# Linear attention and dense experts: one block of down projections per batch in place of two

## The chip, the cores and the metric

The kernel runs on one core of a Trainium2 chip. The metric is the device time of one execution in microseconds (us). TensorE (PE) multiplies matrices, VectorE (DVE), ScalarE (ACT) and GpSimd (POOL) work element by element, and SyncE (SP) mostly issues transfers. Each engine works through its own queue in the order in which the program issues instructions to it, and waits on semaphores for what other engines produce.

## What is computed

For each of 8 batches of 512 tokens with 128 channels (float32):

```python
x = x + layernorm(attention(layernorm(x)))
x = x + layernorm(experts(layernorm(x)))
# attention: k = softmax over tokens; context = k^T v per head; out = q context, then w_out, bias, residual
# experts, for each of 8, with 512 hidden channels:
h = silu(x @ wg) * (x @ wu)
acc = acc + h @ wd
```

No expert is routed: all eight are summed for every token, which is most of the arithmetic.

## The kernel before, in words

The order of all instructions is written out by hand: what the Python code issues first stands first in its engine's queue.

**Steps.** The experts of a batch are cut into 32 steps (8 experts, 4 tiles of 128 hidden channels each). A step is two matmuls of 512 tokens, g (L902) and u (L903), a silu on ScalarE (L905) and a product on VectorE that writes h (L926). g and u have two PSUM banks each. Batch 0 begins with two units of sixteen steps on half of the tokens (256 columns), and then runs steps 16 to 31 on all of them; in the half steps every third step uses the accumulators' banks. The last batch ends with steps 24 to 31 in two halves.

**Down projections.** Steps are taken in pairs, and a 2 by 2 product of a pair is formed with seven block products in place of eight (a Strassen scheme). GpSimd forms sums of the weights once per expert (`weight_sums`, L755) and differences of h for each pair (L940 to L942). The products are matmuls with 64 output channels, two of them side by side (L797, in `down_pairs`), and add up in two banks, accA and accB. `down_pairs` issues a whole block of them: one for the first eight pairs of a batch and one for the rest, each two steps behind its last pair (`LAG`). A batch has two blocks (the last batch one of eight pairs and one of four).

**Work beside the steps.** `plan` gives to each step a list of calls, which are issued behind its product. They prepare the next batches: the first norm of x (`stats`, `scales`, `norm`), its turn to channels (`turn`), the scaling by gamma and beta (`affine`, L493), the keys' product and softmax (`keys`, L501 to L508), the context in four pieces (`context`), the values and the second part of the attention (`values` to `residual`), the norm before the experts and its turn (`stats4` to `turn4`). They also finish the batch before: `Last` turns both accumulators back (`turn`), adds them up (`add`), normalizes and stores (`norm`). A turn is a transpose of 32 by 32 blocks on VectorE (L282, L291, L570), a transfer to DRAM (L270) and four transfers back (L275), all issued by SP. Powers for the norms are GpSimd's (L237, and L238 after it).

**Opening and end.** `opening` runs batch 0's attention by hand in two halves of tokens; its later pieces come from the generator `after_m`, whose second half goes on during the first half steps (the calls `go` in `plan`): statistics, covariance (L648 to L655) with its power (L658), the normalized y with the addition that gives x2 (L661), z from it (L252), the transposes of z (L261). `keep_warm` issues matmuls that nobody reads (L161). `End.finish` normalizes the last half from PSUM and stores it in two pieces.

## Time and profile before

| what | value |
|---|---|
| median of 3 runs | 693.56 us (693.36 to 693.69) |
| the profiled execution | 693.51 us |
| its span in the profile | 691.6 us |
| HBM traffic over the span | 30.82 MB, 45 GB/s |
| transfers to landing: turn out, turn back, x | 2.0 to 2.2, 2.0, 2.8 us |

The profile counts time from the first instruction of its span; the execution has 1.9 us around it. A line of a group or a timeline gives engine, source line, operation, what it writes and reads, partitions by elements, and how often. A matmul of float32 appears as two passes, so a row "x2" of g or u is one matmul. In timelines the first column is the start, the second the duration, both in us, and brackets name the idle time before a row and what ended it; since matmuls overlap, their cost is read from start to start.

### The profile page before, as it was taken

What the parts mean: (1) busy time and instruction counts of PE and PEld (TensorE: products, weight loads), DVE (VectorE), ACT (ScalarE), POOL (GpSimd) and SP (SyncE); (2) the same over time, 40 slices, a digit from 0 to 9 for tenths busy, and PEclk for the clock granted to TensorE, in tenths of its full rate; (3) what the DMA queues carried; (4) which work ended last, traced back from release to release, by engine and by line L of the source; (5) the groups of instructions that cost most, each with busy time, mean ns of one, the idle gap of its engine ahead of it and who ended that gap; (6) DMA issues with size and microseconds to landing.
All of it is one profiled execution on the core that took longest, in us unless ns stands there. A gap on an engine that the chain in (4) does not pass through costs nothing.

```text
span 691.6 us, 9214 instructions
## 1 busy us (share of the span) xinstructions
PE 682.9 (99%) x3175; PEld 374.3 (54%) x3175; DVE 298.3 (43%) x810; ACT 247.9 (36%) x475; POOL 424.6 (61%) x524
## 2 busy tenths in 40 slices
PE   9999999999999999999999999999999999999997
PEld 6786455454554545545455544545445454544576
DVE  6656433543236432563325624256332534134135
ACT  4552441433424333344332434244351423122221
POOL 4779773767548574495726766377673857546521
PEclk9999999999999999999999999999999999999999
DMA  8610201020010200102001010111001010010010
GB/s 265 196 31 1 76 20 58 16 93 0 31 61 1 92 0 31 61 16 78 0 31 61 30 65 0 51 41 57 22 16 63 14 47 1 1 61 1 15 55 24
DMA packets 36672, 30.82 MB, mean 45 GB/s; under 512 B 3985, under 2 KB 28049, under 8 KB 36625
## 3 DMA queue, kind: packets, MB, share of 16 engines
q1 hardware_dynamic: 36336, 30.03, 13.5%
q8 instruction: 25, 0.41, 0.2%
q10 hardware_dynamic: 288, 0.20, 0.1%
q14 instruction: 23, 0.18, 0.1%
HBM read 18.42 MB, written 11.80 MB: 44 GB/s over the span
## 4 chain that ended last, share of the span: by engine, by line
PE 96%; DVE 1%; ACT 1%; DMA 0%; issue 0%; POOL 0%; DVEq 0%; ACTq 0%
PE g L902 32%; PE u L903 31%; PE accA L797 16%; PE accB L797 12%; PE y_ps L528 1%; PE g_ps L443 1%; PE k_ps L501 1%; PE end L699 1%; DMA x<-in_L_attn_x_dram 0%; PE end_A L699 0%; ACT xh L245 0%; PE wa_ps L464 0%; PE end_B L699 0%; PE m_ps L458 0%; PE c_ps L452 0%
## 5 line engine op out<-in xcount | busy, mean ns | idle before, releaser
L926 DVE TENSOR_TENSOR h<-sg,u 128x512 f32<-128x512 f32 (+1 forms) x264 | 172.6, 655 | 352.0 <-PE u L903 340.4
L905 ACT ACTIVATE sg<-g 128x512 f32<-128x512 f32 (+1 forms) x280 | 156.3, 560 | 377.7 <-PE g L902 353.8
L902 PE MATMUL g<-zT,wg 128*128 128x512 f32 (+1 forms) x560 | 267.5, 559 | 1.4 <-ACT sg L905 0.7
L903 PE MATMUL u<-zT,wu 128*128 128x512 f32 (+1 forms) x560 | 265.7, 556 | 0.9 <-DVE h L926 0.9
L940 POOL TENSOR_TENSOR t<-h 128x512 f32<-128x512 f32 x124 | 157.2, 1268 | 158.4 <-DVE h L926 158.4
L903 PEld LDWEIGHTS u<-zT,wu 128*128 128x128 f32 x560 | 106.1, 190 | 115.2 <-issue 109.5
L902 PEld LDWEIGHTS g<-zT,wg 128*128 128x128 f32 x560 | 101.2, 190 | 98.9 <-issue 95.6
L797 PE MATMUL accB<-t,ws 128*64 128x256 f32 x496 | 138.2, 381 | 0.0
L797 PE MATMUL accA<-h,wd 128*64 128x256 f32 x496 | 128.1, 381 | 0.0
L941 POOL TENSOR_TENSOR t<-h,t 128x256 f32<-128x256 f32 x124 | 90.1, 726 | 9.7
L942 POOL TENSOR_TENSOR t<-h,t 128x256 f32<-128x256 f32 x124 | 90.0, 726 | 9.7
L797 PEld LDWEIGHTS accA<-h,wd 128*64 128x64 f32 x496 | 66.6, 137 | 45.2 <-issue 6.4
L797 PE MATMUL accB<-h,ws 128*64 128x256 f32 x248 | 73.8, 379 | 0.0
L797 PE MATMUL accA<-t,ws 128*64 128x256 f32 x248 | 73.8, 379 | 0.0
L797 PEld LDWEIGHTS accB<-t,ws 128*64 128x64 f32 x496 | 66.6, 137 | 0.0
L237 POOL TENSOR_TENSOR rstd<-ve,mhalf 128x4 f32<-128x4 f32 (+1 forms) x28 | 32.8, 1173 | 18.4 <-DVE nm L229 16.3
L797 PEld LDWEIGHTS accB<-h,ws 128*64 128x64 f32 x248 | 34.0, 137 | 17.9
L797 PE MATMUL accB<-t,wd 128*64 128x256 f32 x124 | 36.9, 379 | 0.0
L797 PE MATMUL accA<-t,wd 128*64 128x256 f32 x124 | 36.9, 379 | 0.0
L797 PEld LDWEIGHTS accA<-t,ws 128*64 128x64 f32 x248 | 34.0, 137 | 0.0
L797 PEld LDWEIGHTS accB<-t,wd 128*64 128x64 f32 x124 | 17.0, 137 | 9.0
L516 POOL TENSOR_TENSOR x<-x,bias_sb 128x128 f32<-128x128 f32 x28 | 11.9, 455 | 15.3 <-ACT x L245 15.3
(177 smaller groups left out, 414.3 us busy)
## 6 DMA issues: line engine op xcount, KB each, us to landing
wg<-in_L_ffn_Wg_dram SPq DMA_DIRECT2D x8, 256.0 KB, 6.0
wu<-in_L_ffn_Wu_dram SPq DMA_DIRECT2D x8, 256.0 KB, 5.9
wd<-in_L_ffn_Wd_dram SPq DMA_DIRECT2D x8, 256.0 KB, 6.1
bounce<-f_blkA SPq DMA_DIRECT2D x8, 256.0 KB, 2.0
fA<-bounce SPq DMA_DIRECT2D x32, 64.0 KB, 2.0
bounce<-f_blkB SPq DMA_DIRECT2D x8, 256.0 KB, 2.1
fB<-bounce SPq DMA_DIRECT2D x32, 64.0 KB, 2.0
x<-in_L_attn_x_dram SPq DMA_DIRECT2D x7, 256.0 KB, 2.8
```

The source lines that it names most:

```text
L237: nc.gpsimd.tensor_tensor(rstd, ve, mhalf[:, :n], ALU.pow)
L443: nc.tensor.matmul(g_ps[:, :C], xh[:, j, :], ek[:, :, j * Q : (j + 1) * Q], start=(j == 0), stop=(j == NJ - 1),)
L501: nc.tensor.matmul(k_ps, w_qkv_sb[:, C : 2 * C], self.xnT, start=True, stop=True)
L516: nc.gpsimd.tensor_tensor(self.x1[:, j], self.x1[:, j], bias_sb, ALU.add)
L797: nc.tensor.matmul(o, w, r, start=start, stop=stop)
L902: nc.tensor.matmul(g_ps[:, :cols], wg_sb[e][:, w], zT, start=True, stop=True)
L903: nc.tensor.matmul(u_ps[:, :cols], wu_sb[e][:, w], zT, start=True, stop=True)
L905: nc.scalar.activation(sg[:, :cols], g_ps[:, :cols], AF.Silu)
L926: nc.vector.tensor_tensor(flat(h), sg[:, :cols], u_ps[:, :cols], ALU.mult)
L940: nc.gpsimd.tensor_tensor(t2[:, 0:2], h2[:, 1::2], h2[:, 0:2], ALU.subtract)
L941: nc.gpsimd.tensor_tensor(t2[:, 2], h2[:, 3], t2[:, 0], ALU.subtract)
L942: nc.gpsimd.tensor_tensor(t2[:, 3], h2[:, 2], t2[:, 2], ALU.subtract)
```

## The change

The sixteen pairs of a batch are now all kept (`hp` has 16 buffers for h), and `down_pairs` issues them in one block directly behind step 31 (behind step 23 in the last batch). The differences are formed by a new function `differences`, which writes one of its four results over a part of h that is not read any more; ten pairs are formed during the steps (`EARLY`), the other six inside the block. New in the block are calls of `meanwhile`: the softmax of batch b + 2, the sum, statistics and norm of the batch before, and the bias of batch b + 2. The keys' product of batch b + 2 stands between step 31 and the block; in batch 0 its affine does too. To make room, tiles that had buffers of their own share them (x has two buffers in place of three; y, z, fn, the scratch tiles of turns and others use tags of tiles that are done), and x is loaded later.

The plans change with it: in batch 0 the pieces of the second half move by a step or two, all eight weight sums go to GpSimd at steps 2 to 8 and 10, the softmax of batch 1 goes one step behind its product, and the preparation of batch 2 goes to steps 20 to 30. In the opening, the statistics of batch 1 are issued in single pieces and their moments and powers ahead of m, and the first half of y and z get a bank per piece. In the end, ScalarE subtracts from the mean while the power is formed, and one operation on VectorE scales and adds.

```diff
-    xp = ctx.enter_context(tc.tile_pool(name="xp", bufs=3))
+    xp = ctx.enter_context(tc.tile_pool(name="xp", bufs=2))
+    x2p = ctx.enter_context(tc.tile_pool(name="x2p", bufs=3))
...
-    hp = ctx.enter_context(tc.tile_pool(name="hp", bufs=4))
-    pairp = ctx.enter_context(tc.tile_pool(name="pairp", bufs=9))
+    hp = ctx.enter_context(tc.tile_pool(name="hp", bufs=16))
+    tp = ctx.enter_context(tc.tile_pool(name="tp", bufs=10))
...
+        after = attentions[1] = Attention(1)
+        after.s = bn(after.x[:, :1], "1_1")
...
             nc.vector.tensor_reduce(kmax[:, h : h + 1], k_ps[h][:, :W], AX.X, ALU.max, negate=True)
+            if h == 0:
+                bn(after.x[:, 1:2], "1_1", after.s, 1)
...
+        bn(after.x[:, 2:3], "1_1", after.s, 2)
...
-        after = attentions[1] = Attention(1)
-        after.s = bn(after.x[:, :3], "1_1")
+        bn(after.x[:, 3:], "1_1", after.s, 3)
...
-        bn(after.x[:, 3:], "1_1", after.s, 3)
+        after.sc = scales(after.s, "1_1", pair=True)
+        m = work.tile([P, C], F32, tag="ctxT", name="m_0")
+        ms.append(m)
         nc.vector.tensor_scalar(m, m_ps[:, :C], rsum, None, ALU.mult)
         next(first)
...
-        moment = moments(after.s, "1_1", pair=True)
...
-        after.sc = powers(*moment, "1_1")
...
-        next(first)
...
         def keys(self):
+            self.product()
+            self.softmax()
+
+        def product(self):
             b = self.b
             k_ps = ps.tile([P, N], F32, tag="ps", name=f"k_ps_{b}")
             nc.tensor.matmul(k_ps, w_qkv_sb[:, C : 2 * C], self.xnT, start=True, stop=True)
             kmax = small.tile([P, 1], F32, tag="kmax", name=f"kmax_{b}")
             nc.vector.tensor_reduce(kmax, k_ps, AX.X, ALU.max, negate=True)
-            ekT = work.tile([P, N], F32, tag="ekT", name=f"ekT_{b}")
+            self.k = k_ps, kmax
+
+        def softmax(self):
+            b = self.b
+            k_ps, kmax = self.k
+            ekT = flat(work.tile([P, NQ, P], F32, tag="xhT", name=f"ekT_{b}"))
             ksum = small.tile([P, 1], F32, tag="ksum", name=f"ksum_{b}")
             nc.scalar.activation(ekT, k_ps, AF.Exp, bias=kmax, accum_out=ksum)
...
-        pool, tag = (ps_gu, "u") if lo else (ps, "ps")
-        y_ps = pool.tile([P, N], F32, tag=tag, name=f"y_ps_0_{lo}")
...
+        if lo:
+            y_ps = ps_gu.tile([P, N], F32, tag="u", name=f"y_ps_0_{lo}")
+            y = pieces(y_ps[:, : n * C].rearrange("p (j c) -> p j c", c=C))
+        else:
+            banks = [(ps, "ps"), (ps_acc, "accB")]
+            y = [p.tile([P, N], F32, tag=t, name=f"y_ps_{t}")[:, :C] for p, t in banks]
...
-        for j in range(n):
-            nc.vector.scalar_tensor_tensor(
-                z[:, lo + j], xt[:, lo + j], mvx[:, j, 0:1], y[:, j], ALU.subtract, ALU.mult,
-                accum_out=cov[:, j : j + 1],
-            )
-        nc.vector.tensor_scalar(cov, cov, 2.0 / C, None, ALU.mult)
         nc.vector.reciprocal(rv, ve)
         nc.vector.tensor_tensor(rv, rv, mv[:, :, 1], ALU.mult)
         nc.vector.tensor_tensor(rv, rv, vex[:, :n], ALU.add)
+        for j in range(n):
+            nc.vector.scalar_tensor_tensor(
+                z[:, lo + j], xt[:, lo + j], mvx[:, j, 0:1], y[j], ALU.subtract, ALU.mult,
+                accum_out=cov[:, j : j + 1],
...
         )
         yield
-        norm_apply(z[:, r], x2[:, r], (mvx, rstd2))
-        yield
-        z_ps = transpose4(flat(z[:, r]), f"z_ps_0_{lo}")
-        for j in range(1 if lo else n):
-            cp = nc.vector.tensor_copy if j else nc.scalar.copy
-            if lo:
-                cp(zT[:, :, r], by_block(z_ps[:, : n * P], n))
-            else:
-                cp(zT[:, :, j], z_ps[:, j * P : (j + 1) * P].rearrange("c (a i) -> c a i", a=NQ))
+        if lo:
+            norm_apply(z[:, r], x2[:, r], (mvx, rstd2))
+            yield
+            z_ps = transpose4(flat(z[:, r]), f"z_ps_0_{lo}")
+            nc.scalar.copy(
+                zT[:, r], z_ps[:, : n * P].rearrange("c (j a i) -> c j a i", j=n, a=NQ)
+            )
+        else:
+            for j in range(n):
+                norm_apply([z[:, j]], [x2[:, j]], (mvx[:, j : j + 1], rstd2[:, j : j + 1]))
+                t = (ps_gu if j else ps).tile([P, N], F32, tag="g" if j else "ps", name=f"z_ps_0{j}")
+                nc.tensor.transpose(t[:, :P], z[:, j], ident)
+                (nc.vector.tensor_copy if j else nc.scalar.copy)(
+                    zT[:, j], t[:, :P].rearrange("c (a i) -> c a i", a=NQ)
+                )
...
-            s = [norm_stats([f], f"5_{b}_{self.lo + j}") for j, f in enumerate(self.f)]
+            s = []
             for j, f in enumerate(self.f):
-                norm_apply([fn[:, j]], [f], s[j])
-                (nc.vector if j else nc.gpsimd).tensor_tensor(
-                    o[:, j, :], fn[:, j, :], x2s[b][:, self.lo + j], ALU.add
+                s.append(norm_stats([f], f"5_{b}_{self.lo + j}"))
+
+                nc.scalar.activation(
+                    fn[:, j], f, AF.Identity, bias=s[j][0][:, 0, 0:1], scale=-1.0
+                )
+            for j in range(self.n):
+                nc.vector.scalar_tensor_tensor(
+                    o[:, j, :], fn[:, j], s[j][1], x2s[b][:, self.lo + j], ALU.mult, ALU.subtract,
+                    reverse1=True,
                 )
                 (nc.scalar if j else nc.sync).dma_start(dst[:, self.lo + j], o[:, j, :])
...
-    GROUP = 16
+    FIRST = 16
+    EARLY = 10
...
-    def down_pairs(b, g, pairs):
...
+    def differences(pair):
+
+
+        h = pair[0]
+        t = tp.tile([P, 3, N // 2], F32, tag="t2", name="t2")
+        pair.append(t)
+        nc.gpsimd.tensor_tensor(t[:, 0:2], h[:, 1::2], h[:, 0:2], ALU.subtract)
+        nc.gpsimd.tensor_tensor(t[:, 2], h[:, 3], t[:, 0], ALU.subtract)
+        nc.gpsimd.tensor_tensor(h[:, 1], h[:, 2], t[:, 2], ALU.subtract)
...
+    def down_pairs(b, pairs, calls):
...
+        A, D = sums = [
+            ps_acc.tile([P, N], F32, tag=f"acc{t}", name=f"acc{t}_{b}") for t in "AB"
+        ]
...
-                    below.append((D[low, left], w1[:, high], t[:, 3], False, False))
+                    below.append((D[low, left], w1[:, high], h[:, 1], False, False))
                 else:
-                    above.append((A[high, left], w1[:, high], t[:, 3], False, closes))
+                    above.append((A[high, left], w1[:, high], h[:, 1], False, closes))
...
-        if g * GROUP + 2 * len(pairs) == end:
-            fins[b] = Last(b, accs.pop(b))
+            late = EARLY + two // 2
+            if late < len(pairs):
+                differences(pairs[late])
+            for call in calls.get(two // 2, []):
+                call()
+        fins[b] = Last(b, sums)
...
+        def load(b):
+            if b < B:
+                xs[b] = load_x(b)
+                attentions[b] = Attention(b)
+
+        def differ(k):
+            return lambda: differences(pairs[k])
+
         if b == B - 1 and begin:
             if not lo:
-                at(26, lambda: fins[b].turn_both())
+                at(24, lambda: fins[b].turn_both())
...
                 go = lambda: next(second, None)
                 at(0, go, a.norm)
-                at(1, go)
-                at(3, a.turn)
-                at(4, go)
-                at(6, go)
-                at(8, go)
-                for i, e in enumerate((0, 1, 2, 3, 4)):
-                    at(2 + 2 * i, lambda e=e: weight_sums(nc.gpsimd, [e]))
+                at(2, go)
+                at(4, a.turn)
+                at(5, go)
+                at(7, go)
+                at(10, go)
+                for e in range(E):
+                    at(2 + e if e < 7 else 10, lambda e=e: weight_sums(nc.gpsimd, [e]))
                 at(9, a.bias)
                 at(13, a.affine)
-                at(14, a.keys)
+                at(14, a.product)
+                at(15, a.softmax)
             else:
-                for i in range(12, 16):
+                at(0, lambda: load(2))
+                for i in range(13, 16):
                     at(i, a.context)
-            return p
-
-        second = None
-        if b + 2 < B:
-            second = attentions[b + 2] = Attention(b + 2)
-        if b:
+                for k in range(5):
+                    at(1 + 3 * k, differ(k))
+        elif b == 0:
+            second = attentions[2]
+            at(16, a.context)
+            at(17, a.values)
+            at(18, a.stats3)
+            at(19, a.scales3)
+            at(20, second.stats)
+            at(21, a.residual)
+            at(23, a.stats4)
+            at(24, a.scales4)
+            at(25, second.scales)
+            at(26, a.norm4, a.turn4)
+            at(29, second.norm)
+            at(30, second.turn)
+            for k, i in enumerate((17, 20, 22, 26, 29), 5):
+                at(i, differ(k))
+        else:
             last = lambda name: lambda: getattr(fins[b - 1], name)()
-            at(2, last("turn"))
-            at(3, last("turn"))
+            at(0, last("turn"))
+            at(1, last("turn"))
             if a:
-                at(1, a.keys, a.bias)
-                for i in range(4, 8):
+                for i in range(3, 7):
                     at(i, a.context)
-                at(8, a.values)
-                at(9, a.stats3)
-                at(10, a.scales3)
-                at(12, a.residual)
+                at(7, a.values)
+                at(8, a.stats3)
+                at(9, a.scales3)
+                at(11, a.residual)
+                at(13, lambda: load(b + 2))
                 at(14, a.stats4)
                 at(15, a.scales4)
-            if second:
-                at(17, second.stats, second.scales)
-            if a:
                 at(17, a.norm4, a.turn4)
-            at(17, last("add"), last("stats"), last("scales"))
-            if second:
-                at(17, second.norm, second.turn)
-                at(21, second.affine)
-            at(17, last("norm"))
-        else:
-            at(16, a.values)
-            at(17, a.stats3, a.scales3, second.stats, second.scales, a.residual)
-            at(17, lambda: weight_sums(nc.vector, [5, 6, 7]), second.norm, second.turn)
-            at(19, a.stats4)
-            at(20, a.scales4)
-            at(22, a.norm4, a.turn4)
-            at(24, second.affine)
+            if b + 2 < B:
+                second = lambda name: lambda: getattr(attentions[b + 2], name)()
+                at(19, second("stats"))
+                at(20, second("scales"))
+                at(22, second("norm"))
+                at(23, second("turn"))
+                at(30, second("affine"))
+            for k in range(EARLY):
+                at(2 * k + 1 + (k if b < B - 1 else 0), differ(k))
+        return p
+
+    def meanwhile(b):
+
+
+        a = attentions.get(b + 2)
+        last = lambda name: [lambda: getattr(fins[b - 1], name)()] if b else []
+        p = {i: [] for i in range(6)}
+        p[0] += last("add")
+        if a:
+            p[0] += [a.softmax]
+        p[1] += last("stats") + last("scales")
+        p[5] += ([a.bias] if a else []) + last("norm")
         return p
...
-        if lo == begin == 0 and b + 2 < B:
-            xs[b + 2] = load_x(b + 2)
...
-            made = not last and i % 2 and hi == NJ
-            if made:
-                t2 = pairp.tile([P, 4, N // 2], F32, tag="t2", name=f"t2_{n}_{i}")
-                pairs.append((h2, t2))
-                if len(pairs) == GROUP // 2 or i == end - 1:
-                    due.append((count + LAG, partial(down_pairs, b, i // GROUP, pairs)))
-                    pairs = []
+                if i % 2 and hi == NJ:
+                    pairs.append([h2])
             for call in p[i]:
                 call()
             while due and due[0][0] <= count:
                 due.pop(0)[1]()
...
-                nc.gpsimd.tensor_tensor(t2[:, 0:2], h2[:, 1::2], h2[:, 0:2], ALU.subtract)
-                nc.gpsimd.tensor_tensor(t2[:, 2], h2[:, 3], t2[:, 0], ALU.subtract)
-                nc.gpsimd.tensor_tensor(t2[:, 3], h2[:, 2], t2[:, 2], ALU.subtract)
...
+        if whole:
+            if b + 2 < B:
+                if b == 0:
+                    attentions[2].affine()
+                attentions[b + 2].product()
+            down_pairs(b, pairs, meanwhile(b))
+            pairs.clear()
+            h2s.clear()
```

## The prediction, made before the result was known

> **What bounds the kernel now.** I read the page first (busy table, chain that ended last), then the waits of TensorE, then timelines: TensorE at the edges of a block of down projections, all engines in the first 50 us, and the tail.
>
> ```profile
> PE 682.9 (99%) x3175; PEld 374.3 (54%) x3175; DVE 298.3 (43%) x810; ACT 247.9 (36%) x475; POOL 424.6 (61%) x524
> PE 96%; DVE 1%; ACT 1%; DMA 0%; issue 0%; POOL 0%; DVEq 0%; ACTq 0%
> PE u L903 <- DVE h L926: 0.9, 2, 0.7
> PE g L902 <- ACT sg L905: 0.7, 1, 0.7
> ```
>
> TensorE is busy 99% of the span, and the chain runs 96% through it. Its waits after the opening are two stalls before u (0.9 us) and one before g (0.7 us), all in the first 40 us. The sum therefore goes by what TensorE executes and by what newly stops it. Both kernels issue the same 1594 matmuls in the same shapes (counted in each engine's instruction order), so the work itself saves nothing.
>
> **Blocks: -2.7 us.** Entering and leaving a block:
>
> ```profile
> 139.06 1.02 PE L903 MATMUL u<-zT,wu 128*128 128x512 f32 x2
> 140.01 0.43 PE L797 MATMUL accA<-h,wd 128*64 128x256 f32 x1
> 140.27 0.38 PE L797 MATMUL accA<-h,wd 128*64 128x256 f32 x1
> ...
> 151.94 0.38 PE L797 MATMUL accA<-t,wd 128*64 128x256 f32 x1
> 152.24 1.13 PE L902 MATMUL g<-zT,wg 128*128 128x512 f32 x2
> 153.21 1.02 PE L903 MATMUL u<-zT,wu 128*128 128x512 f32 x2
> ```
>
> Inside the steps a matmul of 512 columns starts 0.86 after the one before; inside a block a pass follows after 0.215. The block starts 0.95 after u (0.09 extra), its second pass 0.26 after the first (0.045 extra), g starts 0.30 after the last pass (0.09 extra), and the next u 0.97 after g (0.11 extra): 0.335 us for each block. The trace has 16 blocks (eight batches, two each), the new order eight: 8 x 0.335 = 2.7 us saved. All 16 measure alike, so this term is sure to 0.1.
>
> **Differences inside the block: 0.** Ten pairs are formed ahead, six during the block, in the order pair 10, pair 11, a power (L237, 1.02 + 0.20), pairs 12 to 15. A triple takes GpSimd 2.9 us (1268 + 726 + 726 ns and gaps). A tile is free about 1.7 us into the block; pair 15 is ready at 1.7 + 6 x 2.9 + 1.3 = 20.4 us. Eight rounds of 3.02 us (critical view: 141.09, 144.11) need it at 7 x 3.02 + 1.3 = 22.4. The cover is 2 us; rival D is its loss.
>
> **Opening: +0.3 us (-0.4 to +0.7).** The moments of batch 1 (four aggregates to two negations, 13.39 to 14.34, 0.95 us on VectorE) now stand ahead of m, which waited for m_ps and started at 13.12. They can start at 12.72, so m starts at 13.67, +0.55. Three small operations also move ahead of the covariance (about +0.1). What comes back is the second zT copy, which sat 0.72 us idle behind the first and now has a bank of its own: about -0.35.
>
> **Weight sums: +2.2 us (1.7 to 2.6).** All eight experts go to GpSimd at steps 2 to 8 and 10, and the x2 addition of the second half (L661) now comes behind three of them; before, behind one.
>
> ```profile
> 24.51 0.69 POOL L658 TENSOR_TENSOR cov<-cov,mhalf 128x2 f32<-128x2 f32 x1
> 25.17 0.46 POOL L755 TENSOR_TENSOR ws<-wd 128x128 f32<-128x128 f32 x1
> ...
> 26.95 0.72 POOL L661 TENSOR_TENSOR x<-yn,x 128x256 f32<-128x256 f32 x1
> ```
>
> VectorE reaches the covariance 0.8 us later (one more h, 0.34, and three small operations, 0.47, go first) and GpSimd saves 0.26 of waiting, so the power starts at 25.05, the sums at 25.7. Three experts of 1.78 (27.63 to 29.41 for one) end at 31.05, the addition at 31.8, VectorE's z (0.99) at 32.75. Queued behind z on VectorE is h of step 8 and all after it; TensorE stands before the transposes of z, which the order has behind step 10. Undisturbed it reaches them at 28.81 + two steps of 0.86 = 30.55. The stall is 2.2. Before, one expert stood ahead of the addition and nothing waited; three put GpSimd's queue into a chain that TensorE waits for.
>
> **Exponential of batch 1: +0.5 us (0.2 to 0.8).** ScalarE's hole (two table loads of 1.28, the exponential, the accumulator read) moves from before to behind the silu of step 15. That ends at 36.2; load, exponential, load, next silu end at 36.24 + 1.28 + 0.6 + 0.2 + 1.28 + 0.38 = 40.0. The first g that needs its bank is four steps behind k_ps, at 35.22 + 4 x 0.86 = 38.67: 1.35 late against 0.87 now.
>
> **Keys of batch 2: +6.45 us (6.1 to 7.3).** This is the large term. In batch 0 the normalized x of batch 2 is turned at step 30; its affine and its product k_ps stand directly behind step 31, ahead of the block. Before, turn and affine were four steps and a whole block apart. The turn goes through DRAM:
>
> ```profile
> 130.67 0.60 ACT L905 ACTIVATE sg<-g 128x512 f32<-128x512 f32 x1 [1.12 <-PE g L902]
> 131.38 1.65 ACT L245 ACTIVATE y<-y,nm,rstd 128x128 f32<-128x128 f32 x4
> 132.93 0.57 ACT L905 ACTIVATE sg<-g 128x512 f32<-128x512 f32 x1
> 133.54 0.69 DVE L926 TENSOR_TENSOR h<-sg,u 128x512 f32<-128x512 f32 x1 [1.25 <-ACT sg L905]
> ```
>
> ```profile
> 68.36 0.34 SPq L270 DMA_DIRECT2D bounce<-xh_blk  x1
> 70.45 1.73 SPq L275 DMA_DIRECT2D xhT<-bounce  x4
> ```
>
> The first fence is the same pattern (four activations of a normalization after one step's silu, step start 129.61): the next h starts 2.2 us into its step. So with S the start of step 30: h at S + 2.2, the turn at S + 2.8 to 3.5 (0.70, L282), bounce issued at S + 3.55, four loads from S + 5.65 (2.09 later), the last issued 1.3 on, landed 2.0 later (DMA list) at S + 8.95, affine 0.80 (L493) to S + 9.85, k_ps at S + 9.9. Two steps end at S + 3.44. Behind k_ps in TensorE's queue stand the whole block and batch 1; nothing covers the 6.45 us. The ends are the shortest and longest bounce (2.03, 2.88) and landing.
>
> **Clock after that gap: +2.5 us (0 to 2.5).** The longest idle time of TensorE after its start is 0.7 us (the waits above), so the trace shows no matmul after a long gap. The nearest row is the start:
>
> ```profile
> 0.77 4.60 PE L161 MATMUL unread<-const-float32-1.0 128*128 128x256 f32 x10 [0.77 <-PEq L966]
> 15.14 0.60 PE L161 MATMUL unread<-x 128*128 128x256 f32 x2
> ```
>
> From rest ten passes of 256 columns take 0.466 each (0.77 to 5.43); later two, of 0.38 each, end within 0.60, so they start 0.22 apart. The cold stretch cost 10 x 0.25 = 2.5 us; at the other end it costs nothing, if a gap this short keeps the rate. I take 2.5. The slices of granted clock show 9 throughout and can't tell. [...]
>
> **Tail: -0.4 us (-0.6 to 0).** After the last power (ends 688.17) now come a scaling (688.20, 0.41), an addition and the DMA at 688.97; afterwards one operation of 0.35 and the DMA near 688.57.
>
> **Hidden.** The eight batches' other moves cost nothing: turns at steps 0 and 1 follow the block as at 2 and 3 before, the x load at step 13 has six steps for 2.8 us, the turn at step 23 has seven steps (12 us) for the 6.3 us to its affine. If a cover goes, the step's 1.72 us is the unit. SP is waited on only in the keys' carry; the shared tiles' readers are done by the order's own distances.
>
> **Sum** on the profiled execution (693.51, span 691.6): -2.7 + 0.3 + 2.2 + 0.5 + 6.45 + 2.5 - 0.4 = +8.85, so 702.4; the median of 693.56 gives the same. Low ends: -2.8 - 0.4 + 1.7 + 0.2 + 6.1 + 0 - 0.6 = +4.2, 697.7. High ends: -2.6 + 0.7 + 2.6 + 0.8 + 7.3 + 2.5 = +11.3, 704.8. Differences under 0.2% can't be told from no change here.
>
> **Rivals.**
> - B: the gap keeps the rate. All else as above: 693.51 + 6.35 = 699.9. For it: the granted clock never moves in any slice. Against: the start does run at half rate.
> - C, not slower: k_ps does not wait, because the carry is back in time. Without 6.45 and 2.5 the sum is -0.1: 693.4. It decides where turn to affine takes less than the two steps that remain: S + 3.44 against a turn that ends at S + 3.5. For it: in the trace nobody waits long for xhT (0.3 us in all). Against: those carries had a block in between.
> - D: the 2 us of cover in the block are not there, because GpSimd runs late: each triple 15% longer ends pair 15 2.6 us later, 0.6 late, and with the norm's power waiting for VectorE about 1 us in seven blocks: 702.4 + 7 = 709. Against: mean durations above already include VectorE beside it.
> - That the change does not do what it says: the order shows one block per batch, so no.
>
> **Chances.** Forecast 0.68; B 0.17; C 0.08; D 0.07. C lies around zero: faster 0.03, same 0.04, slower 0.01. So faster 0.03, same 0.04, slower 0.93. The range takes the forecast's and B's bounds, 698 to 705, and leaves out C, D and a little of each end, 0.2.
>
> **What would show it.** Eight block edges of 0.335; k_ps of batch 2 waiting about 6.5 us for xnT, and passes of 0.4 or more behind it (B: 0.215); the transposes of z waiting about 2 us, with VectorE waiting for GpSimd's x2; the first g about 0.3 later; g in the second half of batch 0 waiting 1.3 for a silu. If k_ps waits under 4 us or TensorE waits in the blocks of batches 1 to 7, the prediction is wrong.

## The result, and the profile after

The changed kernel takes 702.07 us (median of 4 runs, 701.47 to 702.41) against 693.51 for the kernel before in the same runs: a ratio of 1.0123, 95% interval 1.0110 to 1.0135. It is slower by 8.6 us. The profiled execution took 701.76 us with a span of 699.8, 8.2 us more than before.

The page shows how little of this an average shows: TensorE's busy time is the same (682.9 us before), and its share of the chain that ended last fell from 96% to 93%, with 1% each on GpSimd, the transfers and issue, which had 0% before.

```profile
PE 682.7 (98%) x3175; PEld 375.9 (54%) x3175; DVE 299.9 (43%) x797; ACT 246.6 (35%) x477; POOL 429.2 (61%) x535
...
PE 93%; DVE 1%; POOL 1%; ACT 1%; DMA 1%; issue 1%; SPq 0%; POOLq 0%; ACTq 0%; DVEq 0%
```

The waits of TensorE (who waited for whom: us in total, times, longest) name the places. The first two were not there before; the third was 0.7, the fourth 0.9.

```profile
PE k_ps L504 <- ACT xnT L492: 6.1, 1, 6.1
PE z_ps L256 <- DVE z L247: 1.7, 2, 1.4
PE g L965 <- ACT sg L968: 1.2, 1, 1.2
PE u L966 <- DVE h L989: 1.0, 2, 0.8
```

The largest wait, in the timeline of batch 0's end (start, duration, engine, line, operation; the idle time before a row in brackets):

```profile
83.41 1.02 PE L966 MATMUL u<-zT,wu 128*128 128x512 f32 x2
83.43 0.70 DVE L277 STREAM_TRANSPOSE xh_blk<-xh 128x512 f32<-128x512 f32 x1
...
84.16 0.34 SPq L265 DMA_DIRECT2D bounce<-xh_blk  x1
...
86.23 1.73 SPq L270 DMA_DIRECT2D xhT<-bounce  x4
...
89.63 0.81 ACT L492 ACTIVATE xnT<-xhT,beta_sb,gamma_sb 128x512 f32<-128x512 f32 x1 [5.42 <-DMA xhT<-bounce]
...
90.50 2.08 PE L504 MATMUL k_ps<-xnT,w_qkv_sb 128*128 128x512 f32 x2 [6.06 <-ACT xnT L492]
...
92.50 0.69 PE L831 MATMUL accA<-h,wd 128*64 128x256 f32 x1
...
92.98 0.63 PE L831 MATMUL accA<-h,wd 128*64 128x256 f32 x1
```

The last u of the batch is issued while the turn is only starting. The product stands next in TensorE's queue and follows 7.09 us behind u, where 0.86 is normal (174.29 to 175.15 in the next batch): 6.2 us. Then look at the starts behind it: the block's first pass comes 2.00 later, and the next passes at 0.42 us, not 0.215, until 94.25. Every later block has its passes at 0.215.

The second wait, on TensorE, and the starts of the blocks of batches 1 and 2 (changed kernel; the last row is the kernel before, where the block before it starts at 140.01):

```profile
30.94 0.59 PE L966 MATMUL u<-zT,wu 128*128 128x256 f32 x2
...
32.98 0.33 PE L256 MATMUL z_ps<-ident,z 128*128 128x128 f32 x1 [1.45 <-DVE z L247]
...
33.68 0.60 PE L965 MATMUL g<-zT,wg 128*128 128x256 f32 x2
...
176.10 0.43 PE L831 MATMUL accA<-h,wd 128*64 128x256 f32 x1
...
258.87 0.43 PE L831 MATMUL accA<-h,wd 128*64 128x256 f32 x1
```

```profile
223.12 0.43 PE L797 MATMUL accA<-h,wd 128*64 128x256 f32 x1
```

The effects read start against start, for the same instruction in both traces:

| step of the prediction | forecast, us | in the profiled execution, us | read from |
|---|---|---|---|
| blocks | -2.7 | -2.7 | period of a batch 83.11 (140.01 to 223.12) before, 82.77 (176.10 to 258.87) after: 8 x 0.34 |
| opening | +0.3 | +0.5 | first g 19.53, now 20.03 |
| weight sums, z | +2.2 | +2.1 | u at 30.94, first g behind the transposes at 33.68, where 0.65 is normal (30.81 to 31.46 with the weight sums later) |
| exponential of batch 1 | +0.5 | +0.5 | g 0.87 late before, 1.41 now |
| keys of batch 2 | +6.45 | +6.2 | above |
| clock behind it | +2.5 | +1.9 | 3.7 us of work at half rate (granted clock 0.50 from 90.5 to 94.2) |
| tail | -0.4 | -0.6 | last transfer 2.95 behind the last down projection before, 2.57 now; end of span 0.2 nearer |
| two small waits of u for h | 0 | +0.25 | 25.40 and 28.24 |
| sum | +8.85 | +8.15 | span +8.2 |

The medians differ by 8.6: the profiled execution of the changed kernel is 0.3 us shorter than the median of its four.

### The profile page after: what moved, and what is told of

It reads as the page before. It is cut to its first block, busy times and chain, and to the rows that moved or that the text cites. A ratio compares the mean times of both kernels' runs of the same rounds, so it can differ in the third digit from the quotient of the medians.

```text
span 699.8 us, 9265 instructions
## 1 busy us (share of the span) xinstructions
PE 682.7 (98%) x3175; PEld 375.9 (54%) x3175; DVE 299.9 (43%) x797; ACT 246.6 (35%) x477; POOL 429.2 (61%) x535
## 4 chain that ended last, share of the span: by engine, by line
PE 93%; DVE 1%; POOL 1%; ACT 1%; DMA 1%; issue 1%; SPq 0%; POOLq 0%; ACTq 0%; DVEq 0%
PE g L965 31%; PE u L966 30%; PE accA L831 15%; PE accB L831 12%; PE k_ps L504 1%; PE y_ps L536 1%; PE g_ps L442 1%; POOL ws L783 1%; PE end L720 1%; ACT xh L240 0%; DMA x<-in_L_attn_x_dram 0%; PE end_A L720 0%; DMA bounce<-xh_blk 0%; DMA xhT<-bounce 0%; POOL cov L673 0%
## 5 line engine op out<-in xcount | busy, mean ns | idle before, releaser
L831 PE MATMUL accA<-h,wd 128*64 128x256 f32 x620 | 146.5, 381 | 0.0
L831 PEld LDWEIGHTS accA<-h,wd 128*64 128x64 f32 x620 | 84.6, 137 | 41.9 <-PE u L966 3.8
L793 POOL TENSOR_TENSOR h<-h,t 128x256 f32<-128x256 f32 x124 | 90.8, 732 | 9.7
L792 POOL TENSOR_TENSOR t<-h,t 128x256 f32<-128x256 f32 x124 | 90.3, 728 | 9.7
L831 PE MATMUL accB<-h,wd 128*64 128x256 f32 x124 | 36.9, 379 | 0.0
L240 ACT ACTIVATE fn<-q,nm,rstd 128x128 f32<-128x128 f32 x28 | 11.5, 482 | 39.3 <-POOL nm L233 39.3
L240 ACT ACTIVATE x<-x,nm,rstd 128x128 f32<-128x128 f32 x56 | 22.9, 482 | 0.0
L185 POOL TENSOR_TENSOR rstd<-ve,mhalf 128x2 f32<-128x2 f32 (+1 forms) x5 | 3.2, 644 | 31.0 <-DVE ve L183 30.8
```

The costliest lines, as they stand in the source:

```text
L240: nc.scalar.activation(d, t, AF.Identity, bias=nm[:, i : i + 1], scale=rstd[:, i : i + 1])
L792: nc.gpsimd.tensor_tensor(t[:, 2], h[:, 3], t[:, 0], ALU.subtract)
L793: nc.gpsimd.tensor_tensor(h[:, 1], h[:, 2], t[:, 2], ALU.subtract)
L831: nc.tensor.matmul(o, w, r, start=start, stop=stop)
```

## The experiments

The theory is the prediction's: two single stalls in batch 0, the keys' product with a slow clock behind it and the transposes of z, outweigh what eight blocks save. The rivals were a rate that survives the gap, a late GpSimd inside the blocks, and gains that are given back at the next wait.

**The product inside the block**

```diff
         if a:
-            p[0] += [a.softmax]
+            if b == 0:
+                p[2] += [a.affine, a.product]
+            p[0 if b else 3] += [a.softmax]
...
-                if b == 0:
-                    attentions[2].affine()
-                attentions[b + 2].product()
+                if b:
+                    attentions[b + 2].product()
```

> The changed kernel with the affine and the keys' product of batch 2 moved from ahead of the block to behind its third round (9.06 us into it), the softmax behind the fourth; norm and turn stay at 29 and 30. Theory (the only fault of the keys' product is that nothing stands ahead of it while the carry is under way): wait and slow passes both go, 6.19 + 1.9 = 8.1 us: 694.0, less sharp by 0.1 to 0.3 for the product's edges inside the block. Rival (the block itself waits: its first pairs or differences are not ready directly behind step 31): part of the 6 us stays, 696 or more.

Measured 694.00 us (ratio 1.0007, 0.9998 to 1.0016). The turn stayed at step 30; only the place of the product changed, and 8.1 us went. Nothing in the block waits. The carry's 6 us were never the fault; that nothing stood between was.

**The gap filled with matmuls that nobody reads**

```diff
                     attentions[2].affine()
+                    keep_warm(warm, 14)
```

> The changed kernel with 14 matmuls of 256 columns, which nobody reads, issued by TensorE between step 31 of batch 0 and the keys' product of batch 2. They take 14 x 0.43 = 6.0 us, so they lie inside the 6.06 us for which the product waits, and the product starts when it did. Theory (TensorE falls to half rate because it stood idle, and needs some busy time to return): behind the product all passes follow at 0.215, and the 1.9 us that the first 3.75 us of work lost are saved: 702.07 - 1.9 = 700.2. Rival 1 (the first passes of a block are slow for another reason, such as their operands or the transfers beside them): 702.1 and passes still at 0.42. Rival 2 (filling costs more than it saves because the product is late): above 702.1.

Measured 699.85 us. The product started at 90.66 (90.50 in the changed kernel), TensorE was no longer idle ahead of it, the passes behind it came at 0.215, and the granted clock stayed at 1.00 (82 to 98 us). 2.2 us less for 6 us more of work: the slow passes came with the idle time, not with the block.

**The gap shortened by one and by two steps**

The edit for one step; for two, the norm stands at 27 and the turn at 28.

```diff
-            at(29, second.norm)
-            at(30, second.turn)
+            at(28, second.norm)
+            at(29, second.turn)
```

> The changed kernel with the norm and the turn of batch 2 one step earlier (28 and 29). The wait of the keys' product should be shorter by one step of 1.72 us, about 4.4 us in place of 6.1. Theory A (any idle time that long costs the rate): the slow passes stay, 702.07 - 1.72 = 700.35. Theory B (it takes more than 4.4 us of idle time to lose the rate): slow passes go too, 700.35 - 1.9 = 698.45. Rival (the carry is later because another transfer stands ahead of it): no gain, 702.1.

> The changed kernel with the norm and the turn of batch 2 two steps earlier (27 and 28). The wait should be about 2.6 us in place of 6.1. Theory A (the rate is lost after 2.6 us too): 702.07 - 3.44 = 698.6. Theory B (the rate is lost only after a longer idle time): 698.6 - 1.9 = 696.7. Rival (the second norm's four activations now follow directly on the first's in ScalarE's queue and its turn on the other turn in SP's, so that the carry is not earlier): 700 or more.

Measured 700.68 us and 699.88 us. With one step the product started 1.76 earlier, as expected; with two only 2.44. The timeline of the kernel with two shows why:

```profile
79.88 1.74 SPq L270 DMA_DIRECT2D zT<-bounce  x4
...
80.32 0.70 DVE L277 STREAM_TRANSPOSE xh_blk<-xh 128x512 f32<-128x512 f32 x1
...
81.72 0.38 SPq L265 DMA_DIRECT2D bounce<-xh_blk  x1
```

The blocks are turned at 81.02, but SP is issuing the four loads of the other turn until 81.62, and the store stands behind them: the rival with SP's queue was right in part there. In both kernels the rate was lost (theory A; granted clock 0.50 behind the product). But neither time fits a product that starts 1.76 or 2.44 earlier: the medians fell by 1.4 and 2.2, and the spans of the two traces are only 0.9 and 1.5 shorter (698.9 and 698.3 against 699.8). The granted clock tells where the 0.9 us went that are missing in each trace. In half-microsecond slices of the changed kernel (the column before the last two is the granted clock):

```profile
86.50:87.00 0.50, 0.00 (x0) 0.00 (x0) 0.00 (x0) 0.00 (x0) 0.00 (x0) 1.00 0.00 0
87.00:87.50 0.50, 0.00 (x0) 0.00 (x0) 0.00 (x0) 0.00 (x0) 0.00 (x0) 0.89 0.24 73
87.50:88.00 0.50, 0.00 (x0) 0.00 (x0) 0.00 (x0) 0.00 (x0) 0.00 (x0) 0.50 0.59 173
...
93.50:94.00 0.50, 0.50 (x6) 0.31 (x4) 0.00 (x0) 0.50 (x1) 0.00 (x0) 0.50 0.00 0
94.00:94.50 0.50, 0.50 (x8) 0.26 (x6) 0.00 (x0) 0.50 (x1) 0.00 (x0) 0.79 0.00 0
```

The mean of a slice of which a part is at half rate gives the moment: the clock fell at 87.39, while TensorE stood idle, and rose at 94.21. The same reading of every kernel that lost the rate (us; lost is half of the time from the product's start to the return):

| kernel | product starts | clock falls | clock returns | low for | lost |
|---|---|---|---|---|---|
| changed kernel | 90.50 | 87.39 | 94.21 | 6.82 | 1.86 |
| turn one step earlier | 88.74 | 87.23 | 94.06 | 6.83 | 2.66 |
| turn two steps earlier | 88.06 | 86.84 | 93.67 | 6.83 | 2.81 |
| weight sums later (below) | 88.26 | 87.46 | 94.28 | 6.82 | 3.01 |
| opening and softmax (below) | 90.79 | 88.48 | 95.31 | 6.83 | 2.26 |
| less cover (below) | 90.49 | 87.49 | 94.32 | 6.83 | 1.92 |
| 8 matmuls of filling (below) | 91.06 | 90.92 | 94.33 | 3.41 | 1.64 |

In these seven traces the clock is low for 6.82 to 6.83 us or for 3.41, not for a fixed time from the first matmul: it returned 3.71 us behind the product's start in the changed kernel, 6.02 with the weight sums later, 3.27 with 8 matmuls of filling. That it needs some busy time to return, as the theory of the filled gap has it, is not shown. The low stretch was 3.41 only where the product started 0.14 us behind the fall; a start 0.80 us behind it (weight sums later) already met 6.82. With the turn earlier, the product finds more of the low stretch left. With two steps the product is 2.44 earlier but loses 0.95 more: 1.49 less, and the span is 1.5 shorter. With one step 1.76 - 0.80 = 0.96, and the span is 0.9 shorter.

With the turn two steps earlier the clock fell 2.5 us after the end of the last matmul (84.34 to 86.84). The idle time itself does not set the moment: in waits of 6.05 to 6.06 us the clock fell 2.95 us after that end in the changed kernel (84.44 to 87.39), 3.75 with opening and softmax undone (84.73 to 88.48) and 5.25 with the weight sums later (82.21 to 87.46).

**Filling with eight**

The edit against the kernel with 14:

```diff
-                    keep_warm(warm, 14)
+                    keep_warm(warm, 8)
```

> The changed kernel with 8 in place of 14 matmuls that nobody reads ahead of the keys' product of batch 2: 8 x 0.43 = 3.44 us of the wait are filled, 2.6 to 2.7 us stay idle, and the product starts when it did. Theory A (an idle time of 2.6 us does not cost the rate): as with 14, 699.85, and the executions lie within 0.4 us of each other. Theory B (it does): 1.7 to 2.8 us of it are lost again, 701.5 to 702.7, and the executions scatter by about 1 us, as they do in the kernels that have slow passes (702.41 - 701.47, 700.7 - 699.27) and not in the two that have none (700.15 - 699.81, 694.11 - 693.85).

Measured 701.74 us (701.51 to 702.13): theory B. The timeline of TensorE, this kernel:

```profile
84.45 3.65 PE L163 MATMUL unread<-const-float32-1.0 128*128 128x256 f32 x16
91.06 2.07 PE L504 MATMUL k_ps<-xnT,w_qkv_sb 128*128 128x512 f32 x2 [2.96 <-ACT xnT L492]
93.06 0.69 PE L831 MATMUL accA<-h,wd 128*64 128x256 f32 x1
```

An idle time of 3.0 us lost the rate here, 2.8 us after its start (88.10 to 90.92). Not every idle time of 3.0 us must: with the weight sums later the clock stayed up for the first 5.25 us of the wait. 1.45 us, the wait for z, did not lose it: the transposes' followers there are at full rate (granted clock 1.00 from 30 to 34 us in the changed kernel; g to u 0.44, 33.68 to 34.12). Nor did 2.04 us, the wait of a g with opening and softmax undone: the matmuls from it on start 0.54, 0.46 and 0.43 apart (42.42 to 43.85). Between 2.04 and 2.96 us nothing was tried. The scatter that was expected is about half there: 0.6 us against 0.3 with 14.

**The weight sums behind the addition**

```diff
-                    at(2 + e if e < 7 else 10, lambda e=e: weight_sums(nc.gpsimd, [e]))
+                    at(5 + e, lambda e=e: weight_sums(nc.gpsimd, [e]))
```

> The changed kernel with the weight sums of the eight experts on GpSimd at steps 5 to 12 of the first half in place of 2 to 8 and 10, so that the addition that gives the second half's x2 stands ahead of all of them. Theory (three experts ahead of that addition hold up TensorE's transposes of z): the wait there, 1.45 + 0.21 us and 2.09 against an undisturbed step, is gone: 702.07 - 2.1 = 700.0. Rival 1 (the norm's chain is late for another reason, the power of the covariance or VectorE's queue): the wait stays, 702.1. Rival 2 (GpSimd's queue now holds up something later, the differences or the bias): up to 702.1 with a new wait behind step 15.

Measured 700.38 us. The wait before the transposes is gone and no other took its place. The cause, in GpSimd's and VectorE's rows of the changed kernel:

```profile
31.29 0.46 POOL L783 TENSOR_TENSOR ws<-wd,ws 128x128 f32<-128x128 f32 x1
...
31.70 0.73 POOL L676 TENSOR_TENSOR x<-yn,x 128x256 f32<-128x256 f32 x1
...
32.47 0.99 DVE L247 TENSOR_SCALAR z<-x,mv,cov 128x128 f32<-128x128 f32 x2 [3.00 <-POOL x L676]
```

The addition's inputs were there at 28.2; it starts with the end of the twelfth sum. The product of batch 2 started 2.24 earlier, but the time fell by 1.7 only, and the span by 1.1: the table above shows the rest of the span, 1.15 us more lost to the low clock.

**Opening and softmax undone**

```diff
-        after.sc = scales(after.s, "1_1", pair=True)
         m = work.tile([P, C], F32, tag="ctxT", name="m_0")
...
+        moment = moments(after.s, "1_1", pair=True)
         weights = prepare()
...
+        after.sc = powers(*moment, "1_1")
         keep_warm(flat(yn[:, J[0]]), 2)
...
-                at(15, a.softmax)
+                at(14, a.softmax)
```

> The changed kernel with two parts undone that act at different places. First, the moments of batch 1 stand behind m again and their powers later, as before the change. Second, the exponential of batch 1 stands at step 14 again, directly behind its product. Theory: m starts at about 13.1 in place of 13.62 and the first g at 19.4 to 19.6 in place of 20.03 (0.5 us); the g that waits for a silu in the first half steps waits 0.7 in place of 1.24 (0.54 us): together 702.07 - 1.0 = 701.05. Rival for the first (GpSimd, not m, sets the first g, since the powers of batch 1 then stand ahead of the covariance): first g stays at 20.0. Rival for the second (the bank is late for the silu in any order): wait stays 1.2.

Measured 703.71 us (702.44 to 704.40), slower than the changed kernel. The first part did what it should: m at 13.11, first g at 19.55, 0.48 earlier. The second did the opposite: the g waits 2.04 in place of 1.24, though the exponential stands one step earlier. ScalarE's row tells it:

```profile
38.60 1.28 ACT L520 ACT_TABLE_LOAD   x1 [1.71 <-DVE kmax L512]
```

Before the change the load of the table began at 34.49, 0.92 ahead of kmax's start, and only the exponential waited. Here the load waits for kmax too. The exponential now writes the tile that the affine reads, so it has a second thing to wait for. That one of its two waits stands at the load is my reading: the load begins at 38.60, kmax ends at 38.53; the last experiment tries another tile. Step 15 is thus the better place as long as the tile is shared: there kmax is ready before the silu ends.

The profiled execution is the shortest of the four, 702.44. Its span is 0.7 above the changed kernel's, as the two parts (-0.48 and +0.80) and 0.40 more lost to the low clock make it. The other 1.3 us of the median are in no trace; the two longest executions, 704.27 and 704.40, were granted a mean clock of 0.992, the others 0.994 and 0.995, which fits a longer low stretch and is not shown.

**Less cover for GpSimd inside the block**

```diff
-    tp = ctx.enter_context(tc.tile_pool(name="tp", bufs=10))
+    tp = ctx.enter_context(tc.tile_pool(name="tp", bufs=9))
...
-    EARLY = 10
+    EARLY = 9
...
-            for k, i in enumerate((17, 20, 22, 26, 29), 5):
+            for k, i in enumerate((17, 20, 22, 26), 5):
...
-        p[5] += ([a.bias] if a else []) + last("norm")
+        p[0] += [a.bias] if a else []
+        p[5] += last("norm")
```

> The changed kernel with less cover for the differences inside the block: nine pairs formed ahead in place of ten, nine buffers for them in place of ten, and the bias of batch b + 2 (1.70 us on GpSimd) behind the first round in place of the sixth. GpSimd's last triple of a block then ends 2.85 + 1.70 = 4.55 us later. In the trace of the changed kernel the last pair is ready at 196.18 and its last use is at 199.83 (its first part 194.58 for 198.53): a cover of about 3.6 us. By that each of batches 1 to 5 waits 0.95, batches 0, 6 and 7 not: 702.07 + 4.8 = 706.9. By the 2 us of cover of the prediction each of these five waits 2.55 and two others 0.8 to 1.3: 702.07 + 15 = 717. Rival (the differences never hold up TensorE): 702.1.

Measured 713.17 us, 11.1 more than the changed kernel: neither number. Blocks 1 to 5 are 2.16 us longer each (26.48 against 24.32), block 6 by 0.58, the others not. GpSimd's rows at the end of block 1:

```profile
197.85 1.27 POOL L629 TENSOR_TENSOR fn<-fn,x 128x512 f32<-128x512 f32 x1
199.07 1.26 POOL L791 TENSOR_TENSOR t<-h 128x512 f32<-128x512 f32 x1
```

What I had left out: with nine ahead, the last triple comes behind the calls of round 5, and with them behind the addition of the batch's last norm, 1.27. The delay is 4.55 + 1.27 = 5.8; less 3.6 of cover it is 2.2, as measured, and 2.85 + 1.27 - 3.6 = 0.5 in block 6, where 0.58 was measured. This was worked out behind the result, but two kinds of block agree on it: the cover is 3.6 us, and beyond it TensorE waits for GpSimd.

**Blocks of eight steps in the kernel before**

```diff
     def down_pairs(b, g, pairs):
+        GROUP = 8 if b else 16
...
-                if len(pairs) == GROUP // 2 or i == end - 1:
-                    due.append((count + LAG, partial(down_pairs, b, i // GROUP, pairs)))
+                G = 8 if b else GROUP
+                if len(pairs) == G // 2 or i == end - 1:
+                    due.append((count + LAG, partial(down_pairs, b, i // G, pairs)))
```

> The kernel before with blocks of eight steps in place of sixteen in batches 1 to 7: four blocks per batch, three in the last, 13 more in all with the same products. Theory (each block costs 0.335 us for entering and leaving): 693.5 + 13 x 0.335 = 697.9. Rival 1 (what a block costs at its edges is hidden by the steps beside it): 693.5. Rival 2 (the differences of a block's last pair, two steps ahead of it, come late more often): above 698.5, with waits of the down projections for GpSimd.

Measured 698.75 us: 5.3 us for 13 blocks, 0.41 each, with no wait of the down projections. Rival 1 fell, and so did rival 2, though the time lies above its 698.5. The edges themselves measure 0.34 as before (0.95, 0.27, 0.31 and 0.96 in the trace), while the period of a batch grew by 0.82 for two blocks (126.20 to 210.13, against 83.11); where the other 0.07 of a block lies was not found.

**The tail alone, on the kernel before**

```diff
-            s = [norm_stats([f], f"5_{b}_{self.lo + j}") for j, f in enumerate(self.f)]
+            s = []
             for j, f in enumerate(self.f):
-                norm_apply([fn[:, j]], [f], s[j])
-                (nc.vector if j else nc.gpsimd).tensor_tensor(
-                    o[:, j, :], fn[:, j, :], x2s[b][:, self.lo + j], ALU.add
+                s.append(norm_stats([f], f"5_{b}_{self.lo + j}"))
+
+                nc.scalar.activation(
+                    fn[:, j], f, AF.Identity, bias=s[j][0][:, 0, 0:1], scale=-1.0
+                )
+            for j in range(self.n):
+                nc.vector.scalar_tensor_tensor(
+                    o[:, j, :], fn[:, j], s[j][1], x2s[b][:, self.lo + j], ALU.mult, ALU.subtract,
+                    reverse1=True,
                 )
```

> The kernel before with only the end of the change: ScalarE subtracts from the mean while the power is formed, and one operation on VectorE scales and adds. Theory: the last transfer starts 0.4 us earlier against the last down projection, as in the trace of the changed kernel (2.57 us behind it in place of 2.95), and the span ends 0.2 us sooner behind that: 693.5 - 0.4 to 0.6 = 692.9 to 693.1. Rival (the first piece's transfer, not the last, sets the end): 693.5.

Measured 693.11 us against 693.36, ratio 0.9996 (0.9987 to 1.0004): by time it can't be told from nothing. In the trace the last transfer starts 2.57 behind the last down projection, as expected (685.69 to 688.26). The end of the span comes 2.8 us behind that start, against 2.6 in the kernel before and 2.45 in the changed one: the 0.2 that the table counts behind the last transfer is a difference between executions, not the change's.

**Repairs together**

The first is the product inside the block, the sums at 5 to 12, and the moments behind m; the second moves the exponential to step 14 as well, with a tile that is free then:

```diff
-            ekT = flat(work.tile([P, NQ, P], F32, tag="xhT", name=f"ekT_{b}"))
+            ekT = flat(work.tile([P, NQ, P], F32, tag="xhT" if b > 1 else "fB", name=f"ekT_{b}"))
```

> Three repairs together on the changed kernel: the affine and the keys' product of batch 2 inside the block (measured 694.0), the weight sums behind the addition that gives x2 (2.1 us of waiting less), and the moments of batch 1 behind m (first g 0.48 earlier). Theory (the terms add, since they lie at different places of TensorE's queue): 694.0 - 2.1 - 0.48 = 691.4. Rival (a stall ahead only moves to a later wait): 692.5 or more, with the g that waits for a silu, 1.24 us now, longer than that.

> As the run with the three repairs, and the exponential of batch 1 back at step 14, but its result in the tile fB, which is free then, in place of that of the transposed x. Theory (at step 14 with the shared tile, the load of ScalarE's table stood behind the wait for the maximum, 38.53 to 38.60, where before it ran ahead of it, since the tile shared with the affine's input brings a second wait on the exponential): the load runs ahead of the maximum again, the g behind waits 0.7 in place of 1.24: 691.4 - 0.54 = 690.9. Rival (the load waits for the maximum whatever the tile): the g waits 2.0 as in the run with the shared tile at step 14, 692.2.

Measured 691.56 us (ratio 0.9975, 0.9965 to 0.9985) and 691.03 us (0.9966, 0.9954 to 0.9979). In the second the load runs ahead of the maximum again:

```profile
34.98 1.28 ACT L520 ACT_TABLE_LOAD   x1
...
36.63 0.69 ACT L520 ACTIVATE ekT<-k_ps,kmax 128x512 f32<-128x512 f32 x1 [0.37 <-DVE kmax L512]
```

The g behind it waits 0.70. The terms add (691.4 and 690.9 were expected), since they lie one after the other in one queue. With its stalls in batch 0 taken out, the change as a whole beats the kernel before by 0.34%, 2.3 us; 0.4 of that is the tail's, not the blocks'.

## Why the prediction was right, and where its terms were off

It held because the work of TensorE was counted first (equal), so that only edges and new waits were left to price, and each wait was found by what stands behind it in a queue. The largest, of the keys' product, is shown by the run that takes it away and nothing else. That the sum of 702.4 lies 0.3 from the median is in part luck: clock and keys were set 0.85 too high together, the opening and two waits 0.45 too low, and the executions scatter by 0.9.

- **Blocks, -2.7**: 0.34 each in the changed kernel; by the period of a batch. With more blocks it was 0.41 each, so the step is shown in both directions.
- **Differences inside the block, 0**: right, and rival D fell, but the cover was 3.6 us and not 2. I had set the need of the whole last pair at 1.3 us into the last round. By their places in the round only its first difference is needed then (198.60, ready at 194.57); the second (199.03, ready at 195.39) has the least cover, 3.6, and the last, whose end I had right (20.1 us into the block, 20.4 worked out), is needed 1.3 us after the first (199.90, ready at 196.18).
- **Opening, +0.3**: 0.5. m came at 13.62, as worked out (13.67). The power of the covariance began 0.75 later, where m and 0.1 made 0.6, and took 0.97 in place of 0.69; z came 0.97 later, and the banks per piece gave 0.47 of it back, more than my 0.35. The step is sure to some 0.2 us only: the first g lies at 19.45 and 19.53 in two traces with the old opening (blocks of eight steps, the kernel before) and at 19.90, 19.94 and 20.03 in three with the new one (weight sums later, less cover, the changed kernel).
- **Weight sums, +2.2**, and **exponential, +0.5**: 2.1 and 0.54, by the mechanisms named. What the second left out is that the shared tile makes the table's load wait; at step 15 it costs nothing, at step 14 it cost 1.3 us (the g waits 2.04 against 0.70 with another tile).
- **Keys of batch 2, +6.45**: 6.2. The turn began 2.6 us into step 30 where I had 2.8; the rest of the sum stood. Rival C, a carry back in time, fell.
- **Clock, +2.5**: the mis-sized term. That the rate is lost in the gap was right, and rival B (the rate survives) fell; but the price was taken from the start of the kernel as though a fixed stretch of work ran slow. What the traces show is a low stretch, 6.82 us here, that began while TensorE stood idle: the product met 3.7 us of it, a loss of 1.9. In the other kernels of the table the same term was 1.6 to 3.0, in three of them above the high end of 2.5 that the prediction gave it.
- **Tail, -0.4**: 0.4 in the chain, as worked out; the 0.2 behind it differ from execution to execution.

## What to carry to other kernels

When work is moved up against its consumer, look at what stands between them in the consumer's queue, and not at how long the producer takes: the same carry cost 8.1 us ahead of the block and nothing inside it. A wait of 2.96 us on TensorE cost 1.64 us more than its length (filling with eight, lost to the low clock), and part of what was gained by shortening such a wait was given back (2.44 us earlier, 0.95 more lost); filling it, or putting work ahead of the product, took the slow passes away. And before tiles are shared, ask which instruction gets the additional wait.

## What the runs showed of the hardware that was not expected

- The low clock lasted 6.82 to 6.83 us (six kernels of the table) or 3.41 us (one), and began 2.5 to 5.25 us after the end of TensorE's last matmul (84.34 to 86.84, 82.21 to 87.46). Most kernels that meet it scatter more from execution to execution: 0.9 us (changed kernel), 1.4 (turn two steps earlier), against 0.3 in two without it (gap filled with 14; product in the block). That this scatter comes from where the low stretch falls is argued, not shown: only one execution of each kernel has a trace. The mean granted clock of each execution does not decide it: with the turn two steps earlier it is 0.995 in the two longer executions and 0.996 and 0.997 in the two shorter, with the turn one step earlier and with the weight sums later 0.995 in the two longer and 0.994 in the two shorter.
- The granted clock in the record is 1.00 over the first 5 us of the kernel before, where ten passes took 0.466 each (the same matmuls in the filled gap, 28 passes in 6.26 us, took 0.22); it does show the low stretch in the middle, in slices of half a microsecond, where the page's 40 slices have a single 8 in place of a 9.
- A power of 128x2 on GpSimd took 0.97 us, against 0.69 to 0.71 elsewhere in the same trace and in that of the kernel before, with an addition of 128x256 on VectorE starting at the same time (17.61 and 17.60), and 0.96 with the opening undone (17.14 and 17.12). In the kernel before, where the addition began 0.25 us into the power (17.11, 16.86), it took 0.69. It was not tried by itself.
